# Two graph layers on one core: first loads in quarters on two queues, folding of a later, W product first in the next slot, TensorE order as written

## The chip, the cores and the metric

The kernel runs on one core of one Trainium2 chip. The metric is the device time of one execution in microseconds, from the runs of the kernel; a profiled execution has its own time beside its span. A core has five engines that work side by side, each through its own queue of instructions in order: TensorE (PE, matrix products and transposes, which end in PSUM), VectorE (DVE), ScalarE (ACT), GpSimd (POOL) and SyncE (SP). They wait for each other by semaphores. Loads and stores are issued by SP, ACT and POOL and are carried out by the core's DMA engines.

## The reference

The input is x, 128 batches of 128 nodes with 512 features in float32, and an adjacency matrix for each batch. Two layers follow each other, each with a residual and a layer norm. The first is masked attention with 8 heads, the second a graph attention with one head:

```python
# layer 0
q = (inputs @ Wq + bq).reshape(bs, n, N_HEADS, HEAD_DIM)
...
logits = jnp.einsum('bqhd,bkhd->bhqk', q, k) / np.sqrt(HEAD_DIM)
logits = jnp.where(mask, logits, NEG_INF)
attn = jax.nn.softmax(logits, axis=-1)
out = jnp.einsum('bhqk,bkhd->bqhd', attn, v).reshape(bs, n, EMBED_DIM)
x = layernorm(x + relu(out @ Wo + bo))
# layer 1
Wh = jnp.matmul(h, W)
e = e_i[:, :, None] + e_j[:, None, :]      # e_i = Wh a1, e_j = Wh a2
e = jax.nn.leaky_relu(e, negative_slope=ALPHA)
e = jnp.where(adj == 0, MASK_VAL, e)
h_prime = jnp.matmul(jax.nn.softmax(e, axis=2), Wh)
x = layernorm(x + elu(h_prime))
```

## The kernel before, in words

Everything is float32. Each batch is one tile of 128 partitions (nodes) by 512. x and the adjacency come in groups of G = 4 batches (`load`, L48 to L54), each group as one transfer of 1 MB and one of 256 KB on SP's queue, into four buffers. The five weights are one transfer of 1 MB each on ACT's queue (`load_weight`, L64). Small vectors come on POOL's queue.

Ahead of all batches the two halves of the vector a are folded into W (L95 to L111): e_i = (x W) a1 is computed as x (W a1), so for each half DVE multiplies the four chunks of W by a, with a sum for each row (L102, `wa_scr`), copies the four sums to a full tile (`wa_rep`, L105), TensorE transposes it (`pwa`, L108), and DVE copies the result out of PSUM (`wa_bc`, L110). The result is needed by the second half of `attention_output`.

The work on a batch is cut into stages, each a Python function, and `slot(t)` calls them for several batches at once, one slot for each batch, from t = -8. In slot t stand, in the order of the text: scores of batch t (`attention_weights`: product `s`, mask, maximum, eight exponentials at L169, one for each head, and the division on POOL at L172); the transposes of the attention of batch t-1 (`ppT`, copied by ACT to `prT`); the transposes of x of batch t+8 (`pxT`, copied by DVE to `xT`); a quarter of the Q product of the next group (`pqT`, L141, moved out of PSUM to `qT` by ACT, L143); the graph weights of batch t-2 (`pj`, then `e` and `nmax` on DVE, the exponential `at` on ACT, L226); attention times V of batch t-1 (`po`, copied by ACT to `oT`); a quarter of the K product (`pkT`); the transpose of the graph weights (`pat`, copied by DVE to `attT`); the output product of batch t-1 (`py`, L200, and on DVE residual, layer norm and the two dot products with `wa_bc`, L209); graph weights times x (`pz`, copied by ACT to `zT`); the V product (`pv`); and last the product with W of batch t-2 (`ph`, L250), followed by an exponential on ACT (`t`, L254), POOL (`t`, L255), DVE (`y`, L257), POOL (`y`, L258), the layer norm and the store on SP's queue.

Slots -8 to -5 only transpose group 0; slots -4 to -1 also compute its Q, K and V, and transpose group 1. From slot 120 on no x is left to be transposed, from slot 124 on there are no more products for Q, K and V: those last slots are called the tail here.

The order of instructions on each engine is not the order of this text: a scheduler of the language sets it, by its own estimates, within what the data allow. PSUM tiles of one bank come from a pool of four that is used in turn (`ps`), so that each such product also waits until the tile four places earlier in that turn is read out; `s` and `ppT` take two larger tiles in turn. Transfers of SP and ACT together use eight completion semaphores in turn, and each transfer waits until the one eight places earlier has landed.

Of the kernel before, what the change touches and what calls it, by code (L numbers as in the profile page):

```python
# [8 lines left out]
F32 = mybir.dt.float32  # L9
I32 = mybir.dt.int32  # L10
AF = mybir.ActivationFunctionType
ALU = mybir.AluOpType
# [6 lines left out]
def tile_two_graph_layers(ctx: ExitStack, tc: tile.TileContext, x, adj, wq, bq, wk, bk, wv, bv, wo, bo, w, a, out,  # L19
                          n_batch=N_BATCH):  # L20
# [7 lines left out]
    nc = tc.nc  # L28
    P = 128
    D = x.shape[2]  # L30
    NC = D // P
    H = 8
    DH = D // H
    G = 4
# [5 lines left out]
    const = ctx.enter_context(tc.tile_pool(name="const", bufs=1))  # L40
    two = ctx.enter_context(tc.tile_pool(name="two", bufs=2))
    small = ctx.enter_context(tc.tile_pool(name="small", bufs=4))
    ps_big = ctx.enter_context(tc.tile_pool(name="ps_big", bufs=2, space=bass.MemoryType.PSUM))
    ps = ctx.enter_context(tc.tile_pool(name="ps", bufs=4, space=bass.MemoryType.PSUM))


    X, ADJ, MASK, XT, QT, KT, V, PR, PRT, OT, X1, EI, EJ, AT, RI, ATT, ZT = ({} for _ in range(17))

    def load(g):
        X[g] = two.tile([P, G, D], F32, tag="x", name=f"x_{g}", bufs=4)  # L50
        ADJ[g] = two.tile([P, G, P], I32, tag="adj", name=f"adj_{g}", bufs=4)
        b0 = g * G
        nc.sync.dma_start(X[g], x[b0:b0 + G].rearrange("b n d -> n b d"))
        nc.sync.dma_start(ADJ[g], adj[b0:b0 + G].rearrange("b n m -> n b m"))  # L54

    load(0)


    ident = const.tile([P, P], F32, tag="ident", name="ident")
# [1 line left out]
    half = const.tile([P, 1], F32, tag="half", name="half")  # L61
    nc.gpsimd.memset(half, -0.5)

    def load_weight(src, name):  # L64
        t = const.tile([P, NC, D], F32, tag=name, name=name)
        nc.scalar.dma_start(t, src.rearrange("(c p) f -> p c f", p=P))
        return t

    def per_partition(src, name):
        t = const.tile([P, NC], F32, tag=name, name=name)  # L70
        nc.gpsimd.dma_start(t, src.rearrange("(c p) -> p c", p=P))
        return t

    def on_all_partitions(src, offset, name):
        t = const.tile([P, D], F32, tag=name, name=name)
        nc.gpsimd.dma_start(t, bass.AP(tensor=src.tensor, offset=src.offset + offset, ap=[[0, P], [1, D]]))
        return t

    wq_sb = load_weight(wq, "wq")
    wk_sb = load_weight(wk, "wk")  # L80
    wv_sb = load_weight(wv, "wv")
    wo_sb = load_weight(wo, "wo")
    w_sb = load_weight(w, "w")
    bq_sb = per_partition(bq, "bq")
    bk_sb = per_partition(bk, "bk")
    bv_bc = on_all_partitions(bv, 0, "bv")
# [4 lines left out]
    bqs = const.tile([P, NC], F32, tag="bqs", name="bqs")  # L91
    nc.vector.tensor_scalar_mul(bqs, bq_sb, qscale)


    wa_bc = []  # L95
    for s in range(2):
        a_bc = two.tile([P, D], F32, tag="o", name=f"a_bc{s}")
        nc.gpsimd.dma_start(a_bc, bass.AP(tensor=a.tensor, offset=a.offset + s * D, ap=[[0, P], [1, D]]))
        wa = const.tile([P, NC], F32, tag=f"wa{s}", name=f"wa{s}")
        for c in range(NC):  # L100
            scr = two.tile([P, D], F32, tag="y", name=f"wa_scr{s}_{c}")
            nc.vector.scalar_tensor_tensor(scr, w_sb[:, c, :], 1.0, a_bc, op0=ALU.mult, op1=ALU.mult,  # L102
                                           accum_out=wa[:, c:c + 1])
        rep = two.tile([P, NC, P], F32, tag="scr", name=f"wa_rep{s}")
        nc.vector.tensor_copy(rep, wa.unsqueeze(2).to_broadcast([P, NC, P]))  # L105
        p = ps.tile([P, NC, P], F32, tag="ps", name=f"pwa{s}")
        for c in range(NC):
            nc.tensor.transpose(p[:, c, :], rep[:, c, :], ident)  # L108
        t = const.tile([P, D], F32, tag=f"wa_bc{s}", name=f"wa_bc{s}")
        nc.vector.tensor_copy(t, p.rearrange("p c k -> p (c k)"))  # L110
        wa_bc.append(t)  # L111

    def layer_norm(dst, src, name):
        st = small.tile([P, nc.vector.BN_STATS_DIM], F32, tag="st", name=f"st_{name}")
        mv = small.tile([P, nc.vector.BN_AGGR_DIM], F32, tag="mv", name=f"mv_{name}")
        rstd = small.tile([P, 1], F32, tag="rstd", name=f"rstd_{name}")
        nc.vector.bn_stats(st, src)  # L117
        nc.vector.bn_aggr(mv, st)  # L118
        nc.gpsimd.tensor_scalar(rstd, mv[:, 1:2], EPS, None, op0=ALU.add)  # L119
        nc.gpsimd.tensor_tensor(rstd, rstd, half, op=ALU.pow)  # L120
        nc.vector.tensor_scalar(dst, src, mv[:, 0:1], rstd, op0=ALU.subtract, op1=ALU.mult)


    def x_transpose(b):
# [11 lines left out]
    def heads_on_partitions(g, f, store, w_t, bias, scale, name):  # L136
        if f == 0:
            store[g] = two.tile([P, NC, G, P], F32, tag=name, name=f"{name}_{g}")
        p = ps.tile([P, G, P], F32, tag="ps", name=f"p{name}_{g}_{f}")
        for c in range(NC):  # L140
            nc.tensor.matmul(p, w_t[:, c, f * P:(f + 1) * P], XT[g][:, c, :, :],  # L141
                             start=(c == 0), stop=(c == NC - 1))
        nc.scalar.activation(store[g][:, f, :, :], p, AF.Identity, bias=bias[:, f:f + 1], scale=scale)  # L143

    def values(b):
        g, i = divmod(b, G)
        p = ps.tile([P, D], F32, tag="ps", name=f"pv_{b}")
        for c in range(NC):
            nc.tensor.matmul(p, XT[g][:, c, i, :], wv_sb[:, c, :], start=(c == 0), stop=(c == NC - 1))  # L149
        V[b] = two.tile([P, D], F32, tag="v", name=f"v_{b}", bufs=6)  # L150
        nc.vector.tensor_add(V[b], p, bv_bc)
# [43 lines left out]
    def attention_output(b):  # L195
        g, i = divmod(b, G)
        oT = OT.pop(b)
        py = ps.tile([P, D], F32, tag="ps", name=f"py_{b}")
        for c in range(NC):
            nc.tensor.matmul(py, oT[:, c, :], wo_sb[:, c, :], start=(c == 0), stop=(c == NC - 1))  # L200
        o = two.tile([P, D], F32, tag="o", name=f"o_{b}")
        nc.vector.tensor_add(o, py, bo_bc)  # L202
        nc.vector.scalar_tensor_tensor(o, o, 0.0, X[g][:, i, :], op0=ALU.max, op1=ALU.add)  # L203
        X1[b] = two.tile([P, D], F32, tag="x1", name=f"x1_{b}", bufs=4)
        layer_norm(X1[b], o, f"0_{b}")
        for s, store in ((1, EJ), (0, EI)):
            store[b] = small.tile([P, 1], F32, tag=f"e{s}", name=f"e{s}_{b}")
            scr = two.tile([P, D], F32, tag="scr", name=f"scr{s}_{b}")
            nc.vector.scalar_tensor_tensor(scr, X1[b], 1.0, wa_bc[s], op0=ALU.mult, op1=ALU.mult,  # L209
                                           accum_out=store[b])  # L210
# [35 lines left out]
    def graph_output(b):  # L246
        zT = ZT.pop(b)
        p = ps.tile([P, D], F32, tag="ps", name=f"ph_{b}")
        for c in range(NC):
            nc.tensor.matmul(p, zT[:, c, :], w_sb[:, c, :], start=(c == 0), stop=(c == NC - 1))  # L250
        r = RI.pop(b)

        t = two.tile([P, D], F32, tag="t", name=f"t_{b}")
        nc.scalar.activation(t, p, AF.Exp, scale=r)  # L254
        nc.gpsimd.tensor_scalar(t, t, 1.0, -1.0, op0=ALU.min, op1=ALU.add)  # L255
        y = two.tile([P, D], F32, tag="y", name=f"y_{b}")
        nc.vector.scalar_tensor_tensor(y, p, r, t, op0=ALU.mult, op1=ALU.max)  # L257
        nc.gpsimd.tensor_tensor(y, y, X1.pop(b), op=ALU.add)  # L258
        layer_norm(y, y, f"1_{b}")
        nc.sync.dma_start(out[b], y)  # L260


    def slot(t):
        def at(stage, b):
            if 0 <= b < n_batch:
                stage(b)

        i = t % G
        g = t // G + 1
        projecting = 0 <= g < NG  # L270
        if i == 0 and 0 < g + 2 < NG:
            load(g + 2)
        at(attention_weights, t)
        at(attention_weights_t, t - 1)
        at(x_transpose, t + 2 * G)
        if projecting:
            heads_on_partitions(g, i, QT, wq_sb, bqs, qscale, "qT")
        at(graph_weights, t - 2)
        at(attention_values, t - 1)
        if projecting:  # L280
            heads_on_partitions(g, i, KT, wk_sb, bk_sb, 1.0, "kT")
        at(graph_weights_t, t - 2)
        at(attention_output, t - 1)
        at(graph_mix, t - 2)
        if projecting:
            values(t + G)
        at(graph_output, t - 2)

    for t in range(-2 * G, n_batch + 2):
        slot(t)  # L290


# [22 lines left out]
```

## Time and profile before

| | us |
|---|---|
| Median of 3 runs (3028.61 to 3030.41) | 3028.78 |
| Profiled execution, its own time | 3031.17 |
| Its span | 3029.4 |
| TensorE busy (96% of the span) | 2895.0 |
| VectorE busy (49%) | 1499.3 |
| GpSimd busy (33%) | 995.2 |
| ScalarE busy (32%) | 960.7 |

The mean granted TensorE clock of the span was 0.994. A row of the timeline gives the start, the time, the engine, the line, the operation, what it writes and reads, the shapes, and how many instructions were merged; in brackets stands the idle time of the engine ahead of it and what ended it. In the chain of waits "issue" is time in which nothing that the profile shows was waited for. Ends of matrix products are modelled, and a product of 128x128 by 128x512 in float32 is two rows of the trace. Line numbers are those of the kernel before.

### The profile page before, as it was taken

To read this page: it belongs to the slowest core of one execution; us is meant where nothing else is said; L and a number is where in the kernel's file an instruction comes from. 1 tells how busy PE (TensorE), PEld (TensorE's weight loads), DVE (VectorE), ACT (ScalarE), POOL (GpSimd) and SP (SyncE) were. 2 spreads that over 40 slices of the span, in tenths; PEclk is the share of its full clock that TensorE was granted. 3 is DMA by queue.
4 is the path that set the end of the run, shared out by engine and by line. 5 is a ranking of instruction groups with operands and counts; after the bars stand their busy time and mean duration, and the time that the engine had idled before them with its cause. 6 is when DMAs were issued, how large, how long until landed. Compare 5 with 4: busy or idle time off the path is not lost.

```text
span 3029.4 us, 33319 instructions
## 1 busy us (share of the span) xinstructions
PE 2895.0 (96%) x12040; PEld 1497.5 (49%) x12040; DVE 1499.3 (49%) x3125; ACT 960.7 (32%) x3073; POOL 995.2 (33%) x1165
## 2 busy tenths in 40 slices
PE   4999999999999999999999999999999999999996
PEld 2555454545555554554555455455545545555443
DVE  1444545555454454545445454544545454454455
ACT  0333333333333333333333333333333333333332
POOL 0233333333333333333333333333333333333333
PEclk9999999999999999999999999999999999999998
DMA  4000000000000000000000000000000000000000
GB/s 153 4 29 28 27 16 28 28 32 28 25 18 28 28 29 32 22 17 32 28 28 25 18 28 28 32 29 25 15 32 29 28 32 15 24 30 13 11 11 21
DMA packets 55413, 83.93 MB, mean 28 GB/s; under 512 B 3280, under 2 KB 19664, under 8 KB 55248
## 3 DMA queue, kind: packets, MB, share of 16 engines
q1 hardware_dynamic: 52224, 75.51, 7.1%
q10 hardware_dynamic: 2640, 5.24, 0.5%
q8 instruction: 94, 1.54, 0.2%
q0 software_dynamic: 384, 1.05, 0.1%
q14 instruction: 71, 0.58, 0.1%
HBM read 48.24 MB, written 33.55 MB: 27 GB/s over the span
## 4 chain that ended last, share of the span: by engine, by line
issue 24%; DVE 21%; PE 19%; ACT 17%; POOL 17%; DMA 1%; SPq 0%; POOLq 0%; ACTq 0%
PE py L200 15%; ACT pr L169 12%; POOL t L255 8%; DVE st L117 6%; POOL y L258 5%; DVE nmax L166 5%; DVE y L257 3%; DVE o L203 3%; DVE o L202 3%; POOL rstd L120 2%; ACT oT L193 2%; ACT qT L143 2%; ACT at L226 2%; DVE mv L118 1%; POOL rstd L119 1%
## 5 line engine op out<-in xcount | busy, mean ns | idle before, releaser
L169 ACT ACTIVATE pr<-pr,nmax 128x128 f32<-128x128 f32 x1024 | 396.0, 388 | 466.6 <-DVE mv L118 451.6
L141 PE MATMUL pkT<-xT,wk 128*128 128x512 f32 x1024 | 473.1, 605 | 46.2 <-DVE xT L134 46.2
L200 PE MATMUL py<-wo,oT 128*128 128x512 f32 x1024 | 476.5, 608 | 16.9
L250 PE MATMUL ph<-w,zT 128*128 128x512 f32 x1024 | 463.6, 596 | 3.9 <-ACT zT L244 3.8
L255 POOL TENSOR_SCALAR t<-t 128x512 f32<-128x512 f32 x128 | 249.5, 1950 | 654.1 <-ACT t L254 654.0
L141 PE MATMUL pqT<-xT,wq 128*128 128x512 f32 x1024 | 460.9, 593 | 0.0
L149 PE MATMUL pv<-wv,xT 128*128 128x512 f32 x1024 | 460.6, 592 | 0.0
L257 DVE SCALAR_TENSOR_TENSOR y<-ph,ri,t 128x512 f32<-128x512 f32 x128 | 96.1, 751 | 586.8 <-POOL t L255 586.8
L172 POOL TENSOR_TENSOR pr<-pr,tot 128x1024 f32<-128x1024 f32 x128 | 243.2, 1900 | 407.8 <-DVE tot L171 407.8
L254 ACT ACTIVATE t<-ph,ri 128x512 f32<-128x512 f32 x128 | 88.0, 687 | 784.7 <-PE ph L250 774.1
L119 POOL TENSOR_SCALAR rstd<-mv 128x1 f32<-128x1 f32 x256 | 57.1, 223 | 820.5 <-DVE mv L118 820.4
L250 PEld LDWEIGHTS ph<-w,zT 128*128 128x128 f32 x1024 | 195.0, 191 | 248.9 <-issue 243.7
L141 PEld LDWEIGHTS pkT<-xT,wk 128*128 128x128 f32 x1024 | 184.4, 189 | 261.6 <-issue 187.0
L202 DVE TENSOR_TENSOR o<-py,bo 128x512 f32<-128x512 f32 x128 | 88.6, 692 | 446.0 <-PE py L200 446.0
L200 PEld LDWEIGHTS py<-wo,oT 128*128 128x128 f32 x1024 | 185.6, 191 | 226.8 <-issue 186.5
L149 PEld LDWEIGHTS pv<-wv,xT 128*128 128x128 f32 x1024 | 185.2, 190 | 186.5 <-issue 186.3
L141 PEld LDWEIGHTS pqT<-xT,wq 128*128 128x128 f32 x1024 | 184.7, 190 | 184.0 <-issue 183.6
L244 ACT COPY zT<-pz 128x512 f32<-128x512 f32 x128 | 75.0, 586 | 529.5 <-PE pz L242 529.5
L258 POOL TENSOR_TENSOR y<-y,x 128x512 f32<-128x512 f32 x128 | 163.2, 1275 | 111.4 <-DVE y L257 107.9
L169 ACT ACTIVATION_READ_ACCUMULATOR pr<-pr,nmax 128x1 f32 x1024 | 191.4, 187 | 0.0
L182 ACT COPY prT<-ppT 128x1024 f32<-128x1024 f32 x128 | 129.5, 1012 | 188.0 <-PE ppT L180 188.0
L160 PEld LDWEIGHTS s<-kT,qT 64*128 64x128 f32 x2048 | 126.0, 188 | 98.8 <-issue 95.3
(61 smaller groups left out, 3204.4 us busy)
## 6 DMA issues: line engine op xcount, KB each, us to landing
x<-in_x_dram SPq DMA_DIRECT2D x32, 1024.0 KB, 5.1
out_dram<-y SPq DMA_DIRECT2D x128, 256.0 KB, 2.0
adj<-in_adj_dram SPq DMA_DIRECT2D x32, 256.0 KB, 2.8
wq<-in_L_gnn_Wq_dram ACTq DMA_DIRECT2D x1, 1024.0 KB, 10.1
wk<-in_L_gnn_Wk_dram ACTq DMA_DIRECT2D x1, 1024.0 KB, 16.4
wv<-in_L_gnn_Wv_dram ACTq DMA_DIRECT2D x1, 1024.0 KB, 20.8
wo<-in_L_gnn_Wo_dram ACTq DMA_DIRECT2D x1, 1024.0 KB, 15.8
w<-in_L_gnn_W_dram ACTq DMA_DIRECT2D x1, 1024.0 KB, 15.3
```

The source lines that it names most:

```text
L117: nc.vector.bn_stats(st, src)
L141: nc.tensor.matmul(p, w_t[:, c, f * P:(f + 1) * P], XT[g][:, c, :, :], start=(c == 0), stop=(c == NC - 1))
L149: nc.tensor.matmul(p, XT[g][:, c, i, :], wv_sb[:, c, :], start=(c == 0), stop=(c == NC - 1))
L166: nc.vector.tensor_reduce(nmax, pr, AX.X, ALU.max, negate=True)
L169: nc.scalar.activation(pr[:, h, :], pr[:, h, :], AF.Exp, bias=nmax[:, h:h + 1], scale=1.0, accum_out=tot[:, h:h + 1])
L172: nc.gpsimd.tensor_tensor(pr, pr, tot.unsqueeze(2).to_broadcast([P, H, P]), op=ALU.mult)
L200: nc.tensor.matmul(py, oT[:, c, :], wo_sb[:, c, :], start=(c == 0), stop=(c == NC - 1))
L202: nc.vector.tensor_add(o, py, bo_bc)
L250: nc.tensor.matmul(p, zT[:, c, :], w_sb[:, c, :], start=(c == 0), stop=(c == NC - 1))
L255: nc.gpsimd.tensor_scalar(t, t, 1.0, -1.0, op0=ALU.min, op1=ALU.add)
L257: nc.vector.scalar_tensor_tensor(y, p, r, t, op0=ALU.mult, op1=ALU.max)
L258: nc.gpsimd.tensor_tensor(y, y, X1.pop(b), op=ALU.add)
```

## The change

Group 0 of x is loaded batch by batch, in four transfers. Each weight is loaded in four transfers of 128 rows; wq and wv stay on ACT's queue, wk, wo and w move to SP's. The folding of a becomes a function that is called ahead of slot -1. In `slot`, the graph output (`ph`) of a batch is called one slot later, as the first stage of that slot, and the graph weights (`pj`) move ahead of the Q product; one more slot is added at the end. The slots run inside a block in which TensorE's instructions keep the order in which they are written; the other engines are still scheduled.

```diff
+        if g == 0:
+            for i in range(G):
+                nc.sync.dma_start(X[g][:, i, :], x[i])
+        else:
+            nc.sync.dma_start(X[g], x[b0:b0 + G].rearrange("b n d -> n b d"))
         nc.sync.dma_start(ADJ[g], adj[b0:b0 + G].rearrange("b n m -> n b m"))
...
-    def load_weight(src, name):
+    def load_weight(src, name, queue):
         t = const.tile([P, NC, D], F32, tag=name, name=name)
-        nc.scalar.dma_start(t, src.rearrange("(c p) f -> p c f", p=P))
+        for c in range(NC):
+            queue.dma_start(t[:, c, :], src[c * P:(c + 1) * P, :])
         return t
...
+    wq_sb = load_weight(wq, "wq", nc.scalar)
+    wk_sb = load_weight(wk, "wk", nc.sync)
+    wv_sb = load_weight(wv, "wv", nc.scalar)
+    wo_sb = load_weight(wo, "wo", nc.sync)
+    w_sb = load_weight(w, "w", nc.sync)
...
+    def fold_a_into_w():
+        for s in range(2):
...
+        at(graph_output, t - 3)
         at(attention_weights, t)
         at(attention_weights_t, t - 1)
         at(x_transpose, t + 2 * G)
+        at(graph_weights, t - 2)
         if projecting:
             heads_on_partitions(g, i, QT, wq_sb, bqs, qscale, "qT")
-        at(graph_weights, t - 2)
         at(attention_values, t - 1)
...
         at(graph_mix, t - 2)
         if projecting:
             values(t + G)
-        at(graph_output, t - 2)
-
-    for t in range(-2 * G, n_batch + 2):
-        slot(t)
+
+    with tc.manual_schedule(engines={mybir.EngineType.PE}):
+        for t in range(-2 * G, n_batch + 3):
+            if t == -1:
+                fold_a_into_w()
+            slot(t)
```

The body of `fold_a_into_w` is that of L95 to L111, unchanged.

More of the change, by code (lines that the diff above doesn't have):

```diff
@@ L52, in load @@
         b0 = g * G
-        nc.sync.dma_start(X[g], x[b0:b0 + G].rearrange("b n d -> n b d"))
+        if g == 0:
[3 more added lines that the diff above has]
+            nc.sync.dma_start(X[g], x[b0:b0 + G].rearrange("b n d -> n b d"))
         nc.sync.dma_start(ADJ[g], adj[b0:b0 + G].rearrange("b n m -> n b m"))
@@ L77, in on_all_partitions @@
         return t
[L79 to L83, printed above, removed]
+    wq_sb = load_weight(wq, "wq", nc.scalar)
[3 more added lines that the diff above has]
+    w_sb = load_weight(w, "w", nc.sync)
     bq_sb = per_partition(bq, "bq")
@@ L92, in tile_two_graph_layers @@
     nc.vector.tensor_scalar_mul(bqs, bq_sb, qscale)
[L95 to L111, printed above, removed]
     def layer_norm(dst, src, name):
@@ L121, in layer_norm @@
         nc.vector.tensor_scalar(dst, src, mv[:, 0:1], rstd, op0=ALU.subtract, op1=ALU.mult)
+    wa_bc = []
+    def fold_a_into_w():
+        for s in range(2):
+            a_bc = two.tile([P, D], F32, tag="o", name=f"a_bc{s}")
+            nc.gpsimd.dma_start(a_bc, bass.AP(tensor=a.tensor, offset=a.offset + s * D, ap=[[0, P], [1, D]]))
+            wa = const.tile([P, NC], F32, tag=f"wa{s}", name=f"wa{s}")
+            for c in range(NC):
+                scr = two.tile([P, D], F32, tag="y", name=f"wa_scr{s}_{c}")
+                nc.vector.scalar_tensor_tensor(scr, w_sb[:, c, :], 1.0, a_bc, op0=ALU.mult, op1=ALU.mult,
+                                               accum_out=wa[:, c:c + 1])
+            rep = two.tile([P, NC, P], F32, tag="scr", name=f"wa_rep{s}")
+            nc.vector.tensor_copy(rep, wa.unsqueeze(2).to_broadcast([P, NC, P]))
+            p = ps.tile([P, NC, P], F32, tag="ps", name=f"pwa{s}")
+            for c in range(NC):
+                nc.tensor.transpose(p[:, c, :], rep[:, c, :], ident)
+            t = const.tile([P, D], F32, tag=f"wa_bc{s}", name=f"wa_bc{s}")
+            nc.vector.tensor_copy(t, p.rearrange("p c k -> p (c k)"))
+            wa_bc.append(t)
     def x_transpose(b):
```

## The prediction

> **What bounds it now.** I read the page first (sections 1, 2, 4), then the waits of TensorE by stretch, then the timeline of the start, of one slot in the middle and of the last slots.
>
> Sections 1 and 2 of the page:
> ```profile
> PE 2895.0 (96%) x12040; PEld 1497.5 (49%) x12040; DVE 1499.3 (49%) x3125; ACT 960.7 (32%) x3073; POOL 995.2 (33%) x1165
> PE   4999999999999999999999999999999999999996
> PEclk9999999999999999999999999999999999999998
> ```
> TensorE is busy everywhere but in the first and the last slice, and only there is its clock or its share low. So the kernel is a start, some 124 even slots, and a tail. The timeline of the start:
> ```profile
> 32.72 0.68 DVE L102 SCALAR_TENSOR_TENSOR wa_scr<-w,a_bc 128x512 f32<-128x512 f32 x1
> ...
> 39.94 4.47 PE L133 MATMUL pxT<-ident,x 128*128 128x128 f32 x20
> ```
> The first useful work waits for w, the last weight, and then for the folding. pqT, the first full product, starts at 44.34 us and runs on without a hole. In the middle, slots repeat every 23.0 us (py at 1508.51, 1531.52). The chain of waits through one:
> ```profile
> 1520.83 1.95 POOL t L255
> 1522.78 0.03 issue
> 1522.81 0.76 DVE y L257
> 1523.57 0.07 issue
> 1523.64 1.29 POOL y L258
> 1524.93 0.02 issue
> 1524.95 0.69 DVE st L117
> 1525.64 1.12 DVE nmax L166
> 1526.76 0.10 DVE mv L118
> 1526.86 3.17 ACT pr L169 x16
> ...
> 1531.00 0.48 ACT oT L193
> 1531.48 0.04 issue
> 1531.52 3.71 PE py L200 x8
> ```
> It is a loop: ph ends, then t, y, nmax, eight exponentials, oT, py, pz, pv, and the next ph. TensorE lacks 0.4 us before pkT and about as much between pat and py; the slot is as long as the loop. The tail is where full products stop. Three of its rows:
> ```profile
> 2961.71 1.09 PE L190 MATMUL po<-prT,v 128*64 128x128 f32 x16
> ...
> 2964.78 3.60 PE L200 MATMUL py<-wo,oT 128*128 128x512 f32 x8
> ...
> 2983.06 5.57 PE L200 MATMUL py<-wo,oT 128*128 128x512 f32 x8
> ```
> The same py takes 3.6 us or 5.57; the second follows three holes in TensorE, of 1.8, 1.6 and 1.1 us. From 2920 us on the mean granted clock is 0.82 (the table of windows).
>
> [...] adj of group 0, in 512 B pieces, was issued at 1.22 and landed at 16.4, while the 1 MB wq beside it landed at 10.8. [...] 370 to 387 GB/s between 10 and 30 us with all engines taken, whichever queues were live.
>
> **Part 1, the loads.** All loads up to the third x are 11.5 MB, and the order decides who lands first. In the built program SP issues x0 (quarters), adj0, wk, wo, w, and only then x1; ACT issues wq and wv. Each transfer of these two queues also waits for the one eight places earlier to land. That leaves six to eight quarters, 1.5 to 2 MB, in flight, some 4 us of data at 375 GB/s, so I expect no lasting hole. The first transpose of x1 stands ahead of pqT on TensorE. So pqT waits for x1, and so for 8.66 MB: SP 5.5 (x0 1.05, adj0 0.26, three weights 3.15, x1 1.05), ACT 2.1, POOL 1.05. In the trace of before that much had been moved by 26.1 us (the table of windows: 193, 330, 371, 387 and 370 GB/s in five stretches of 5 us, 8.26 MB, then 378); about 1 us to landing (the last load landed at 35.8, with 1 GB/s from 35 on) gives 27.1. Bounds: 26.5 with one queue at the 400 GB/s of a lone x, 31 if slow adj0 holds back the quarters behind it (wo's first waits for it).
>
> pqT then starts at 27.1+0.6 = 27.7, on a cold TensorE: before, 20 cold transposes (4.47 us, 0.21 each against 0.11 warm) had warmed it for pqT. [...] I take 2.5. **Gain of the start: 44.3−27.7−2.5 = 14.1.**
>
> **Part 2, folding.** Its DVE work (8 x 0.61 and two copies of 0.42, 5.7 us) goes between w's landing (about 24.5) and x1's copy; that copy is needed only by the transpose after pqT, pkT and pv, 10.3 us after pqT's start, so nothing. Its eight transposes now stand in the stream: 8 x 0.11, with hand-over 0.9 us lost. adj1's and adj2's masks are queued on DVE before V's additions; adj2 lands near 32, V is needed at 38, so nothing. Start in all: **−13.2** (−9.5 to −15.5).
>
> **Part 3, ph one slot later but first.** The written order was "…pv, ph | s, ppT…"; it becomes "…pv | ph, s, ppT…", the same sequence. In the built program ph keeps its place in the middle and the DVE and POOL orders around it stay, so the loop stays: nothing. PSUM buffers keep their turn too (pkT still takes that of pxT).
>
> **Part 4, graph weights ahead of Q.** pj starts 3.4 us sooner; its input was done at 1516.9 and TensorE reaches it at 1522.4, so it does not wait. ACT now makes at before qT: pat 0.57 earlier, but oT follows both as before, so py stays. Only in the slots with a mask is at's input (DVE done at 1529.98) not there when the exponentials end (1529.95): some 0.12 lost in 29 slots, **+3.5** (0 to 4).
>
> **Part 5, order as written.** In the middle the order was the written one already. In the tail it was not: the scheduler put pieces of later s and ppT into the waits. Now they stand ahead of pj, po, pat and py, and TensorE waits. One tail slot from ph's start, with the distances of the slot at 1516.37: ACT t 3.68, POOL 4.46, y 6.44, scores' predicated copy 7.10, statistics 8.58, nmax 9.19, exponentials 10.49 to 13.59, at, pat at 14.1 (14.68 less qT's 0.57). s, ppT, pj and po are over by 7.9, so TensorE is idle for 6.2 us and turns cold in every slot. Then pat to py 0.47 (2935.83 to 2936.30), py cold 4.98 or 5.41 (to pz at 2941.28 and 2988.47), pz to the next ph 1.78 (2988.47 to 2990.25): 14.1+0.5+5.2+1.8 = 21.6. Warm it would be 14.1+0.2+3.4+1.8 = 19.5. Before, four such steps took 2990.25−2920.52 = 69.7; after, 4 x 21.6 = 86.4: +16.7 (warm +8.3; at worst 22.6 each, +20.7). The next slot has no exponentials: pat waits behind y at 8.6, then py, pz, next ph at 14.1, before 11.4 (2990.25 to 3001.61): +2.7 (to +4.6). The last, ph to ph, 10.1 against 10.8: −0.7; the end after it is the same. **Tail: +18.7** (+10 to +25).
>
> **Sum.** −13.2+3.5+18.7 = +9.0. The profiled execution took 3031.17 (span 3029.4 and 1.8 around it), 2.4 above the median of the runs, 3028.78; both kernels bear the same, so I add to the median: **3037.8**. About 0.2%, 6 us, is what a measurement of this kernel can tell from no change.
>
> **Rivals.**
> A: the tail stays warm. The hole of 2.0 us before ph at 2957.97 did not halve the clock[...]. Tail +10: 3029.1, no change.
> B, the other side: the start alone decides. If DVE's or ACT's order let exponentials run ahead, so that pat does not wait for them, the slot falls to what TensorE and ph's round trip need: tail +0, −13.2+3.5: 3019.1, faster. It decides once the tail loses less than 4 us. Against it: ACT's built order has all eight exponentials ahead of at in every tail slot.
> C: x1 is late. With each transfer waiting for the eighth before it, SP could be held up at adj0 and run dry; each us is a us. At 33: start −7.4, total +14.8: 3043.6.
> D: the new order does nothing in the middle. I hold this myself (parts 3, 4), so most of what the change says it moves stays put; were the loop shortened by the 0.4 us before pkT, 120 slots would give −48. Nothing in the orders shortens it; 2 in 100.
>
> **How the numbers follow.** The case of the sum 0.55, C 0.15, A 0.2, B and D 0.1. In the case of the sum about 0.9 lies over +6; C whole; A within or just above; so slower 0.68, same 0.24, faster 0.08. The range drops B and D below, and the worst of C above: low 3026 (A with the best start), high 3047 (tail +25, start −10, +3.5). The likeliest case alone: 3033 to 3043.
>
> **What would show it.** pqT's first matmul at 27 to 31 us, released by x1; slots of 23.0 us in the middle, with 0.4 us before pkT still there, and at right after the exponentials; in the last 130 us four ph 21 to 22 us apart, a hole of about 6 us before pat in each, released by ACT at, and py of 5 us or more. It is wrong if ph are under 18 us apart there, if pqT starts after 35, or if the middle slot leaves 22.9 to 23.1.

## The result, and the profile after

| | before | after |
|---|---|---|
| Median of 4 runs each, us | 3028.7 | 3040.53 (3039.79 to 3041.19) |
| Ratio after to before | | 1.0038 (95% interval 1.0020 to 1.0055) |
| Profiled execution, us | 3031.17 | 3040.50 |
| Its span, us | 3029.4 | 3038.7 |

The changed kernel is slower, by 11.8 us between the medians and 9.3 us between the profiled executions. That is small, but clear of the spread: before was run 60 times more beside the experiments below and never took more than 3033.80 us; after never took less than 3039.79. Line numbers of after are seven larger than those of before in the slots (`py` is L207 instead of L200, `ph` L257 instead of L250).

The page of after, sections 1 and 2 (busy time of each engine; busy tenths of TensorE and its granted clock in 40 slices):

```profile
PE 2886.1 (95%) x12040; PEld 1492.4 (49%) x12040; DVE 1495.2 (49%) x3125; ACT 962.1 (32%) x3073; POOL 995.3 (33%) x1165
...
PE   6999999999999999999999999999999999999975
...
PEclk9999999999999999999999999999999999999997
```

The first digit of the PE row went from 4 to 6, so the start got denser. The last two went from 96 to 75, so the tail got emptier. The clock of the last slice goes from 8 to 7, but over the tail as a whole the granted clock is 0.82 before and after. All instructions of TensorE are still there (12040). The difference has to be looked for at both ends.

I cut each profiled execution at the same two points, the start of the first `ph` and the start of the `ph` of batch 121 (the last before the tail). Both are read from the timeline.

| stretch, us | before | after | difference |
|---|---|---|---|
| to the first `ph` | 135.25 | 121.84 | −13.41 |
| first `ph` to `ph` of batch 121 | 2785.27 | 2786.65 | +1.38 |
| `ph` of batch 121 to the end | 108.87 | 130.20 | +21.33 |

**The start**, timeline of after:

```profile
27.25 1.09 PE L140 MATMUL pxT<-ident,x 128*128 128x128 f32 x4 [15.79 <-DMA x<-in_x_dram]
28.13 5.80 PE L148 MATMUL pqT<-xT,wq 128*128 128x512 f32 x8
33.77 3.60 PE L148 MATMUL pkT<-xT,wk 128*128 128x512 f32 x8
```

TensorE waits 15.79 us for x of group 1 and for nothing else. It is then cold, which means here that it works at half of its full speed, as where the granted clock is 0.50 (at the full one it is called warm): the weight loads of `pqT` come every 0.85 us up to 32.40 and about every 0.43 us from 32.91 on. From the start of `pqT` to that of `pkT` it is 5.64 us, where the next products take 3.4. In before, TensorE's first instruction was the transpose of the folding:

```profile
36.35 1.09 PE L108 MATMUL pwa<-ident,wa_rep 128*128 128x128 f32 x4 [36.35 <-DVE wa_rep L105]
```

By then wq (10.82) and x of group 1 (21.82) had long landed; TensorE waited for the folding, and the folding for w (31.69). In after x of group 1 lands at 27.12, which is 5.3 us later than in before.

**The tail**, TensorE's timeline of after, one slot from `ph` to `ph`:

```profile
2908.49 3.60 PE L257 MATMUL ph<-w,zT 128*128 128x512 f32 x8
2912.02 1.16 PE L167 MATMUL s<-kT,qT 64*128 64x128 f32 x16
2913.11 1.09 PE L187 MATMUL ppT<-ident,pr 128*128 128x128 f32 x8
...
2915.36 1.09 PE L197 MATMUL po<-prT,v 128*64 128x128 f32 x16 [1.05 <-ACT prT L189]
2922.61 0.48 PE L240 MATMUL pat<-ident,at 128*128 128x128 f32 x1 [6.15 <-ACT at L233]
2922.88 5.68 PE L207 MATMUL py<-wo,oT 128*128 128x512 f32 x8
...
2930.18 3.70 PE L257 MATMUL ph<-w,zT 128*128 128x512 f32 x8 [0.73 <-ACT zT L251]
```

All of `s` and all of `ppT` are done by 2914, and then TensorE has nothing that it may do in the order as written. It idles for 6.15 us before `pat`, and `py`, most of it at half clock (the granted clock is 0.50 from 2920.24 to 2927.07), takes 5.68 us (3.60 at full clock). In the tail of before the scheduler had left rows of `s` and `ppT` for such holes, as here ahead of `pat`:

```profile
2932.05 1.65 PE L160 MATMUL s<-kT,qT 64*128 64x128 f32 x10
2935.83 0.47 PE L233 MATMUL pat<-ident,at 128*128 128x128 f32 x1 [2.13 <-ACT at L226]
2936.30 5.14 PE L200 MATMUL py<-wo,oT 128*128 128x512 f32 x8
```

This `py` is cold too (0.50 from 2928.99 to 2939.23). What ended the idle time, from the waits of TensorE in the tail of after (us in all, times, longest):

```profile
PE pat L240 <- ACT at L233: 26.6, 5, 6.2
...
PE pat L240 <- DVE st L103: 2.9, 1, 2.9
```

The wait for `at` alone is 26.6 us in five slots; in the tail of before (2920 to 3013 us) it was 7.6 us in five, the longest 2.3. All waits of TensorE that the profile lists in the tail are 19.6 us in before and 40.7 in after, and these 21.1 us are the loss: its busy time there is 78.7 us before and 78.9 after. `at` is late because it stands behind the eight exponentials of the scores on ScalarE. The chain of waits shows them, and next to nothing between them and `pat`:

```profile
2918.99 3.18 ACT pr L176 x16
2922.17 0.39 ACT at L233 x2
2922.56 0.04 issue
2922.61 0.48 PE pat L240
```

**The middle** keeps its 23.0 us a slot, and the wait in front of `pkT`. In before that wait was 41.2 us in 104 slots between 300 and 2700 us; the waits of TensorE in the same stretch of after:

```profile
PE pkT L148 <- DVE xT L141: 41.3, 104, 0.4
PE py L207 <- ACT oT L200: 25.3, 104, 0.5
```

The second line is new, and costs nothing: `pat` now comes earlier, `py` does not, so the gap between them has grown.

### The profile page after: what moved, and what is told of

It reads as the page before. It is cut to its first block, busy times and chain, and to the rows that moved or that the text cites. A ratio compares the mean times of both kernels' runs of the same rounds, so it can differ in the third digit from the quotient of the medians.

```text
span 3038.7 us, 33449 instructions
## 1 busy us (share of the span) xinstructions
PE 2886.1 (95%) x12040; PEld 1492.4 (49%) x12040; DVE 1495.2 (49%) x3125; ACT 962.1 (32%) x3073; POOL 995.3 (33%) x1165
## 4 chain that ended last, share of the span: by engine, by line
issue 24%; DVE 21%; PE 19%; ACT 18%; POOL 17%; DMA 1%; POOLq 0%; ACTq 0%
PE py L207 16%; ACT pr L176 12%; POOL t L262 8%; DVE st L103 6%; POOL y L265 5%; DVE nmax L173 5%; DVE y L264 3%; DVE o L209 3%; DVE o L210 3%; POOL rstd L106 2%; ACT qT L150 2%; ACT oT L200 2%; ACT at L233 1%; DVE mv L104 1%; POOL rstd L105 1%
## 5 line engine op out<-in xcount | busy, mean ns | idle before, releaser
L207 PE MATMUL py<-wo,oT 128*128 128x512 f32 x1024 | 482.8, 615 | 31.4 <-ACT oT L200 31.2
L257 PE MATMUL ph<-w,zT 128*128 128x512 f32 x1024 | 462.4, 594 | 4.4 <-ACT zT L251 4.4
L207 PEld LDWEIGHTS py<-wo,oT 128*128 128x128 f32 x1024 | 188.4, 194 | 287.6 <-issue 190.5
L257 PEld LDWEIGHTS ph<-w,zT 128*128 128x128 f32 x1024 | 194.7, 191 | 248.5 <-issue 242.9
```

## The experiments

My theory: the change is three things that add up. The loads and the folding win about 13 us at the start, the edits to the slot's text are worth next to nothing, and keeping TensorE's order costs about 20 us in the tail, part of it as waits and part as lost clock. The rival: the tail's loss comes from the moved stages (`ph` first, `pj` earlier), or the two ends are tied through the buffers, so that undoing one would change the other. Each experiment is told with the same stretches as above, from one profiled execution. Each ratio is to runs of before that were made beside it (medians 3029.27 to 3029.51 us).

### e1: the change without the kept order

```diff
-    with tc.manual_schedule(engines={mybir.EngineType.PE}):
-        for t in range(-2 * G, n_batch + 3):
+    for t in range(-2 * G, n_batch + 3):
```

> The changed kernel without the block that keeps TensorE's order. Theory (start gains 13.4, middle loses 1.4, the kept order loses 21 in the tail): the tail gets its interleaved order back and takes 109 us from ph of batch 121 to the end instead of 130; time 3017 (3014 to 3020). Rival (ph called first in the next slot, or the graph weights ahead of Q, make the tail long): tail stays near 130, time near 3040.

Measured: 3018.33 us (5 runs), ratio to before 0.9967 (0.9954 to 0.9980). Start 120.97, middle 2786.02, tail 108.72.

The start's gain is kept in full and the tail is back at the 108.87 of before. Moved stages without the kept order cost nothing there.

### e2: the kept order alone

```diff
-    for t in range(-2 * G, n_batch + 2):
-        slot(t)
+    with tc.manual_schedule(engines={mybir.EngineType.PE}):
+        for t in range(-2 * G, n_batch + 2):
+            slot(t)
```

This is made in the kernel before; nothing else is changed.

> The kernel before with the block that keeps TensorE's order, and nothing else of the change. Theory: start and middle as before, tail 130 us instead of 109, with holes of 6 us before pat; time 3050 (3046 to 3053). Here at comes after exponentials on ACT as well. Rival (the order alone does nothing, since it was the written one already in all slots with products): 3029.

Measured: 3053.19 us (4 runs), ratio 1.0080 (1.0065 to 1.0095). Start 134.61, middle 2784.99, tail 130.59. TensorE's timeline of e2 in the tail:

```profile
2933.70 0.47 PE L233 MATMUL pat<-ident,at 128*128 128x128 f32 x1 [6.15 <-ACT at L226]
2933.97 5.82 PE L200 MATMUL py<-wo,oT 128*128 128x512 f32 x8
```

It is the same hole, to a hundredth, and the same cold `py`, without any other part of the change. Its six distances from `ph` to `ph` in the tail (21.82, 21.20, 22.55, 21.51, 17.25 and 10.55 us) are those of after within 0.13. The kept order by itself makes the whole loss. The time came out just above the forecast range, whose top was 3053.

### e3: the start alone

Loads in quarters on two queues and the later folding, with the slot and the scheduling of before:

```diff
     for t in range(-2 * G, n_batch + 2):
+        if t == -1:
+            fold_a_into_w()
         slot(t)
```

> Loads in quarters on two queues and the folding at slot -1, all else as in the kernel before. Theory: first full product at 28 us instead of 44, first ph 13.4 us sooner, middle at 23.02 us for each slot, tail 109: time 3015 (3013 to 3018), and about 1.4 less than the changed kernel with a scheduled TensorE. Rival (the transfers of the start delay something later, or the folding in the stream costs more than its 0.9 us): above 3019.

Measured: 3018.79 us (5 runs), ratio 0.9962 (0.9948 to 0.9976). Start 121.55, middle 2786.25, tail 111.05.

It is e1's time within the spread of either (3017.41 to 3020.83, 3015.75 to 3020.62). So moving `ph` and `pj` in the text buys nothing that can be measured. The forecast missed, though: 3013 to 3018 was expected. The profiled execution was the slowest of the five, and its tail is 2.3 us longer than that of e1. Of the change, only the start is worth keeping.

This run takes the loads and the folding together. The landings above speak for the folding: with the old loads all that `pqT` and the transposes ahead of it need had landed by 21.82, and the new order of the loads brings x of group 1 later. So the folding alone, with the loads as they were, may well win more than 13 us. That was not run.

### e4: the tail with the clock held up

Behind `po` in slots 124 to 127, six products of the identity with a piece of wq go to a PSUM tile that nobody reads:

```diff
+    def keep_clock(b):
+        p = ps.tile([P, D], F32, tag="ps", name=f"pwarm_{b}")
+        for k in range(6):
+            nc.tensor.matmul(p, ident, wq_sb[:, k % NC, :], start=True, stop=True)
...
         at(attention_values, t - 1)
+        if t >= n_batch - G:
+            at(keep_clock, t)
```

> The changed kernel with six more products of the identity with a piece of wq (128x128 by 128x512, 5.1 us in all, result unused) behind po in slots 124 to 127. Theory (half of the tail's loss is the halved clock after the hole): py falls from 5.5 to 3.5 us, four ph distances from 21.7 to 19.5, time 3032 (3030 to 3034). Rival (py is long because it waits for its inputs): no gain, or the added products delay pat: 3040 or more.

Measured: 3032.24 us (20 runs), ratio 1.0009 (1.0003 to 1.0016). Start 121.82, middle 2786.63, tail 123.08. TensorE's timeline of e4 in the tail:

```profile
2916.34 5.42 PE L194 MATMUL pwarm<-wq,ident 128*128 128x512 f32 x12
2922.57 0.33 PE L245 MATMUL pat<-ident,at 128*128 128x128 f32 x1 [0.81 <-ACT at L238]
2922.73 3.60 PE L212 MATMUL py<-wo,oT 128*128 128x512 f32 x8
```

`pat` starts at the same time as in after (2922.57 against 2922.61), so the useless work delays nothing. `py` is warm. The slots fall to 19.50, 19.60, 19.61 and 19.60 us, the 19.5 that the prediction worked out for a warm tail. These four are 8.5 us shorter than in after. The slot after them, which has no dummies, takes 0.9 us more than in after (18.17), the end 0.5 more, so the tail gains 7.1.

So half clock costs the tail of after at least these 7 us. It is not what after lost against before, though: before was at half clock as much (a mean of 0.82 in both tails; of the whole span 0.994 in before, 0.992 in after, 0.997 in e4), and the loss is the 21.1 us of waits. The dummies win back clock that before loses as well.

### e5: x of group 1 ahead of wo and w

```diff
     wv_sb = load_weight(wv, "wv", nc.scalar)
+    load(1)
...
-        if i == 0 and 0 < g + 2 < NG:
+        if i == 0 and 1 < g + 2 < NG:
```

> The changed kernel with group 1 of x and its adjacency issued on SP after wk, ahead of wo and w. Theory (the first full product waits for x1, and x1 for the bytes ahead of it on its queue): 2.1 MB less ahead at 390 GB/s, so x1 lands at 22 us and pqT starts at 22.5 to 23.5 instead of 28.1, all later stages 5 us sooner: 3035.5 (3033.5 to 3037.5). Rival (a weight or the folding is what counts, since w now lands later): no gain, 3040 or more.

Measured: 3033.2 us (20 runs), ratio 1.0012 (1.0005 to 1.0019). Start 115.14, middle 2786.03, tail 129.57. The timeline of e5:

```profile
21.78 1.09 PE L141 MATMUL pxT<-ident,x 128*128 128x128 f32 x4 [10.78 <-DMA x<-in_x_dram]
22.66 4.57 PE L149 MATMUL pqT<-xT,wq 128*128 128x512 f32 x8
```

x of group 1 lands at 21.65, about where the loads of before had it (21.82), and its transpose starts 5.5 us sooner. `pqT` is less cold too (4.57 us in its row instead of 5.80), and the first `ph` comes 6.7 us sooner. That confirms what sets the start in after: the bytes that are queued ahead of x of group 1. The change left 1 MB of wo and 1 MB of w ahead of it, though they are needed later. The time is 0.3 us better than the forecast range.

### e6: one step of the loop on another engine

If the middle is the loop through `t`, `y`, `nmax`, the exponentials and `oT`, then shortening one link of it must shorten each slot, until TensorE's own work is the bound.

```diff
-        nc.gpsimd.tensor_scalar(t, t, 1.0, -1.0, op0=ALU.min, op1=ALU.add)
+        nc.vector.tensor_scalar(t, t, 1.0, -1.0, op0=ALU.min, op1=ALU.add)
```

> The changed kernel with the step t = min(t,1)-1 on VectorE instead of GpSimd (1.95 us there, about 0.7 here), same mathematics. Theory (the middle is bound by the loop ph, t, y, nmax, exponentials, oT, py): the loop is 1.3 us shorter, TensorE's waits before pkT and py go, and the slot falls from 23.03 to TensorE's own 22.1 to 22.3, some 120 slots: -90 to -112, and 1.3 less in each of four tail slots; time 2935 (2922 to 2952). Rival (TensorE is the bound of the middle, its 0.9 us are no waits but hand-over): slot stays at 23.0, time 3035 to 3041.

Measured: 2913.37 us (4 runs), ratio 0.9619 (0.9605 to 0.9633). Start 121.16, middle 2667.10, tail 123.63. Timeline of e6 in the middle:

```profile
1404.79 0.43 DVE L262 TENSOR_SCALAR t<-t 128x512 f32<-128x512 f32 x1 [2.62 <-ACT t L261]
```

The step takes 0.43 us on VectorE (the 0.7 expected was an estimate) instead of 1.95 on GpSimd. The slot falls from 23.02 to 22.06 us. Between 300 and 2700 us the profile lists no wait of TensorE at all, neither the one before `pkT` nor the one before `py`: from `po` to `pkT` it is 1.03 us instead of 1.49, from `pat` to `py` 0.11 instead of 0.53. The link gave 1.5 us and the slot took 0.96 of it: the rest is now slack, because TensorE has become the bound. The loop was the right reading of the middle. The gain was forecast too small: 2922 us was the best that the range allowed, with slots of 22.1 to 22.3.

### e7: the parts that win, together

e1, e5 and e6 in one kernel.

> x1 ahead of wo and w, t on VectorE, and TensorE's order scheduled as in the kernel before (not kept). Theory: start -18.5, middle -90 to -112, tail as before or some us shorter, against the kernel before: 2910 (2896 to 2925). Rival: the scheduler makes another order once t is elsewhere, and the middle does not keep the 22.2 us of the kept order: above 2935.

Measured: 2885.56 us (4 runs), ratio 0.9528 (0.9512 to 0.9543). Start 115.27, middle 2667.10, tail 99.33. The page:

```profile
PE 2838.6 (99%) x12040; PEld 1489.8 (52%) x12040; DVE 1551.0 (54%) x3253; ACT 973.6 (34%) x3073; POOL 753.6 (26%) x1037
```

Adding the three effects to after gives 3040.5−22.2−7.3−127.2 = 2883.8, so they are independent within 2 us. As in e6, the time is below the forecast range (2896 to 2925). TensorE is busy 99% of the span. This is the fastest version here.

### e8 and e9: a warm start

Dummy products (identity by pieces of wq) ahead of the first transpose of group 1, 14 in e8 and 8 in e9, to take the cold 2.2 us out of `pqT`:

```diff
+    def warm_start(n):
+        for k in range(n):
+            if k % NC == 0:
+                p = ps.tile([P, D], F32, tag="ps", name=f"pwarm_{k}")
+            nc.tensor.matmul(p, ident, wq_sb[:, k % NC, :], start=True, stop=True)
...
+            if t == -G:
+                warm_start(14)    # e9: 8
```

> The changed kernel with 14 products of the identity with pieces of wq (result unused) between the transposes of group 0 and the first transpose of group 1. Theory (the first pqT runs at half clock after 16 us without work): pqT falls from 5.6 to 3.5 us, all else as in the changed kernel: 3038.4 (3037 to 3039.5). Rival: the added products end after x1 has landed and delay pqT: 3040.5 or more.

> Changed kernel with 8 dummy products (identity by pieces of wq, results unused) ahead of the first transpose of the second group, where e8 had 14. Theory (pqT's 2.2 us over a warm 3.43 are TensorE's clock alone): the dummies start at about 16.9 as in e8 and end near 26.4, before that x lands at 27.1; pqT starts at 28.1 to 28.3 as without them and takes 3.4 us instead of 5.64; the first product with W comes near 119.7 instead of 121.84, the kernel at 3038.3. Rival (the gap of some 0.7 us before the transpose, or the mask behind which the transposed x waits, takes it back): pqT over 5 us or later than 29, kernel at 3040.5 or more.

Measured, e8: 3041.58 us (4 runs), ratio 1.0042 (1.0027 to 1.0057), start 123.30, tail 130.58. e9: 3038.56 us (9 runs), ratio 1.0027 (1.0017 to 1.0037), start 119.29, middle 2786.42, tail 131.08. Timelines, first of e8, then of e9:

```profile
15.77 0.43 DVE L142 TENSOR_SCALAR mask<-adj 128x512 int32<-128x512 int32 x1 [7.63 <-DMA adj<-in_adj_dram]
16.85 14.67 PE L135 MATMUL pwarm<-wq,ident 128*128 128x512 f32 x28 [5.14 <-DVE xT L147]
```

```profile
16.85 9.68 PE L135 MATMUL pwarm<-wq,ident 128*128 128x512 f32 x16 [5.66 <-DVE xT L147]
...
27.78 3.60 PE L154 MATMUL pqT<-xT,wq 128*128 128x512 f32 x8
```

e8 lost, by my own sizing. The first dummy needs a PSUM tile that VectorE reads out (a copy of xT), and that copy is queued on VectorE behind the mask of group 0, which starts at 15.77, when its adjacency has landed. So the dummies began at 16.85, and 14 of them ran 4 us past the landing of x. With 8, `pqT` starts at 27.78 and is over in 3.44 us instead of 5.64. The first `ph` comes 2.55 us sooner than in after, which is the cold loss of 2.2 and 0.35 of an earlier start.

### e10: the loop's step moved in the kernel before

The edit of e6, made in the kernel before (L255), with nothing else.

> Kernel before with one step moved from GpSimd to VectorE: t = min(t,1)-1 after the exponential of the graph output. Theory (the slot in the middle is the loop through that step in both kernels alike): middle slots 22.06 us as in e6, the stretch from the first product with W to that of batch 121 2667 us instead of 2785; start as before (first product with W at 135), tail shorter by up to 10 us as in e7 against e1 (99.3 against 108.7), so 2901 to 2912 us. Rival (the gain needs the changed kernel's order of the stream): middle over 2690, kernel over 2925.

Measured: 2902.53 us (4 runs), ratio 0.9579 (0.9564 to 0.9593). Start 134.07, middle 2667.11, tail 100.54.

The middle is that of e6 and e7 to 0.01 us. So the slot in the middle depends on none of the orders tried here, the written or the scheduled, with the stages moved or not. e7 is ahead of e10 by its start (115.27 against 134.07) and by 1.2 us of tail.

## Why the prediction was right, and which terms were off

The kind and place of each effect came out as forecast. The sum was forecast as +9.0, and the profiled executions differ by +9.3, but that it is so close is luck: the middle was forecast 2.1 us too high and the tail 2.6 us too low. Step by step:

**Part 1, loads: right.** x of group 1 landed at 27.12 us (forecast 27.1), and `pqT` started at 28.13 (forecast 27.7). The cold loss was 2.2 (5.64 us against 3.43; the 2.5 forecast was my estimate), with `pqT` at half speed up to 32.40; in e9, with dummies ahead of it, `pqT` took 3.44. Rival C, x held up by the slow adjacency, did not come: wo's first quarter did wait for adj of group 0 (landed at 15.60, wo issued at 15.62), but the loads went on without a break (342, 367, 386 and 388 GB/s in the four stretches of 5 us from 5 to 25 us), and x of group 1 came within 0.1 us of the time worked out without such a hold-up. One reading of the prediction is off: the 11.5 MB of all loads hold four groups of x, not three. No step rests on it.

**Part 2, folding: right in what it costs.** The eight transposes stand at 62.12 to 62.99 in TensorE's stream, 0.87 us (forecast 0.9). Start in all −13.4 against −13.2. What the prediction did not ask is how much of this the folding would have won without the new loads (see e3).

**Part 3, `ph` first: right.** The middle stayed, and e1 and e3, with and without the moved stages, have the same time. Rival D's gain of 48 us (the wait before `pkT` gone) did not come: the wait is there as before, 41.3 us in 104 slots.

**Part 4, +3.5 in the middle: mis-sized, measured +1.4.** I took the wait of `at` for `nmax` in the slots with a mask as 0.12 us. These are the two rows concerned, on VectorE and then on ScalarE (timelines of after, in a slot with a mask):

```profile
1516.83 0.28 DVE L231 TENSOR_REDUCE nmax<-at 128x1 f32<-128x128 f32 x1
```

```profile
1517.21 0.40 ACT L233 ACTIVATE at<-at,nmax 128x128 f32<-128x128 f32 x1
```

`nmax` is done at 1517.11, and ScalarE goes from the exponentials to `at` at 1517.21 without idle time, so `at` hardly waits. `pj` 3.4 us sooner let VectorE take the first step of `e` ahead of the mask, so that `nmax` is done 13.48 us after the start of `ph` instead of 13.61; I had used the time of the old order. A slot with a mask is 0.03 us longer, some 0.8 in all. The other 0.6 are two slots of 23.32 us. Slots of that length stand in the traces of e1, e3, e4, e5, e8 and e9 as well, whatever the order, but not in before or e2. So they go with the loads or the folding; what makes them is open.

**Part 5, the tail: right in kind, +21.3 instead of +18.7.** The four slots were forecast as 4 × 21.6 = 86.4 and measured 21.69, 21.14, 22.51 and 21.50, together 86.84. That TensorE would turn cold in each was an assumption; it did, for 6.83, 6.83, 10.25 and 6.82 us. The slot after them was forecast as 14.1, taking it as warm, and took 17.24. That is the term that was mis-sized. There `pat` waits for VectorE (2.9 us, the second line of the waits above) and starts 9.8 us after `ph`, where 8.6 was forecast: VectorE's copy of `e` into `at` (L229) took 1.27 us there, against about 0.30 in the other slots. GpSimd was adding x to `y` in that time (3002.71 to 3003.97); whether that is the reason was not tested. TensorE is cold again after the wait (0.50 from 3005.58 to 3008.99), and `py` takes 5.2. I had chosen the warm end, and the bound that I had written (+4.6) was too low as well: this slot lost 5.9. The distance after that was 10.56 (forecast 10.1), and the end after the last `ph` 15.56 instead of 16.97, where I expected no difference: the last `ph` falls less into a cold stretch (0.50 for its first 2.9 us, against 5.3 in before) and takes 5.14 us against 6.33. In sum 17.1+5.9−0.3−1.4 = +21.3.

**Rival A** (the tail stays warm) would need slots of 19.5 us, which only the dummy products of e4 gave. **Rival B** (the start alone decides) would need the exponentials behind `at`; the chain shows them ahead of it. Its time, 3019.1, is nearly that of e1 and e3, since they are what it describes: the change without the loss in the tail.

**The median.** I added the sum to the median of before, where the profiled execution had been 2.4 us above its median. After's profiled execution was at its median. So +9.0 became 3037.8 where 3040.5 was measured: of the 2.7 us missing, 2.4 are that offset, which the two kernels did not share, and 0.3 the sum.

## What to carry to other kernels

An order written by hand cost nothing here where every stage had filling products behind it, and 21 us in the last six slots, where they ran out: check it there, and hand the tail back to a scheduler or write a tail of its own. At the start, look first for work that stands ahead of the first full product without being needed by it (here the folding, which waited for the last weight), then order the loads by what that product needs, in bytes ahead of it. When an engine is 96% busy and still has a small hole in every round, follow the loop behind the hole: one link moved to another engine (1.95 to 0.43 us) was here worth nine times the gain of the start.

## What the runs showed of the hardware that I had not expected

**Half clock after short holes.** In the tail of before no hole of TensorE was longer than 2.66 us, and still its granted clock fell to 0.50 at 2928.99, 2976.78 and 3007.50, for 10.24 us each time. From the timeline:

```profile
2929.00 1.22 PE L160 MATMUL s<-kT,qT 64*128 64x128 f32 x6 [2.66 <-DVE pr L163]
2930.14 1.97 PE L190 MATMUL po<-prT,v 128*64 128x128 f32 x16
...
2957.97 3.70 PE L250 MATMUL ph<-w,zT 128*128 128x512 f32 x8 [1.98 <-ACT zT L244]
```

`po` takes 1.97 us after the first hole (1.09 elsewhere), while over the hole of 1.98 us the granted clock is 1.00, and `ph` after it takes 3.70 us. The fall at 2976.78 came after a hole of only 1.78 us. So in these runs the length of the last hole alone does not decide it; what does was not shown.

**GpSimd on one input.** Here `t`, one float32 input of 128x512 with two operations, took 1.95 us on GpSimd and 0.43 on VectorE, 4.5 times as long. This step, on the chain of waits, did not belong on GpSimd.
